# A scan's own-pixel term moved from VectorE passes to matrix products in PSUM

## The chip, the core and the metric

The kernel runs on one core of a Trainium2 chip. The metric is the device time of one execution in microseconds (us), the median of several runs. The core has five engines that run side by side and meet through semaphores: PE (TensorE: matrix products, which read SBUF and write PSUM; its weight loads are shown as PEld), DVE (VectorE), ACT (ScalarE), POOL (GpSimd) and SP (SyncE, which here issues the DMAs). Every array is float32.

## The reference

Four layers work on 32 images of 192 channels and 56 x 56 pixels, each of the form x = x + layer(group norm(x)): agent attention, a bidirectional RWKV scan, a shifted small convolution, and a long convolution by spectra. The change is in the second layer. Cut to what matters:

```python
k, v, r = xs @ Wk.T, xs @ Wv.T, xs @ Wr.T          # xs: the normalised image, one row per pixel
def wkv_scan(w, u, k, v):                           # over the pixels t, for each channel
    y[t]  = (p + exp(u + k[t]) * v[t]) / (q + exp(u + k[t]))
    p     = exp(w) * p + exp(k[t]) * v[t]
    q     = exp(w) * q + exp(k[t])
x_bi = 0.5 * (wkv_scan(forwards) + wkv_scan(backwards))
h    = layer_norm(sigmoid(r) * x_bi) * ln_g + ln_b
out  = h @ Wo.T
```

(The reference also carries a running maximum, left out here.) So at a pixel the numerator is the running sum p of the pixels before it plus exp(u) times its own term exp(k) v, and the denominator is the running sum q plus exp(u) times exp(k).

## The kernel before, in words

`all_blocks` runs, one after the other: `make_filter`, `attention` (over images), `scan_pairs` (the second layer), a guarded version of it that is skipped unless numbers overflow, and `channel_blocks` (third and fourth layer together). The change is within `scan_pairs`.

`scan_pairs` takes the images two at a time, 16 pairs. The 384 channels of a pair make three tiles of 128 partitions: the first 128 channels of either image, and the last 64 of both together. The 3136 pixels are cut into 4 pieces (m) of MC = 784, so a tile is 128 x 784, and as a PSUM bank holds 512 numbers, a product over a tile is two halves of 392 (HM). `turned()` hands out a PSUM buffer of two banks, one half in each; there are four such buffers.

Matrix products over channels go through `_Pairs`: `outer` makes the first two tiles, with a 128 x 128 block for each (L860) and a 64-row block for the shared tile (L863); `inner` makes the third, with a 128 x 128 block (L870) and 128 x 64 blocks (L873).

For each pair and piece there are three parts:

- `forwards`: normalised x (L1052, on ACT), key products and exp (L1101: ek = exp(k)), value products times ek (L1106: bv = exp(k) v), then for each tile `scan` forwards, `inverse` of the denominator, and the product num x den into y (L1113).
- `backwards`: normalised x again, the gate's products and its sigmoid as exp, ln, exp (L1126, L1130, L1131), `scan` backwards over the kept ek and bv, `inverse`, num x den (L1134), added to y (L1135) and times the gate (L1136).
- `finish`: centring products of y, squares (L1149), mean products, ln (L1158) and exp (L1168) for the layer norm, output products, the scale (L1169), the sum onto x (L1170), bn_stats of the result (L986), and the stores.

`scan` does the same twice, for p (from bv) and for q (from ek): POOL copies the carried value into the edge column of a fresh tile z of 785 columns (L1065), DVE runs the scan (L1070), POOL copies the last column out as the carry (L1071), and DVE makes `src * eu + before` in place over the columns "before" each pixel (L1072), with eu = exp(u) of each channel. `inverse` makes 1/den on ACT as exp(-ln den) (L1077, L1078), and keeps a sum of it for the overflow check. The z tiles have five buffers (tag pq), the x tiles seven, the tiles of tag t (gate, squares, rd) eight.

The main loop runs over pairs p. In each of its four turns it writes `backwards` of a piece of pair p, `finish` of the piece before it, `forwards` of a piece of pair p + 1, and in the first two turns `measure`, the moments of pair p + 2. No order is written by hand beyond that: a scheduler sets the order of each engine's instructions from the program's order, the dependences and the free buffers, once, when the kernel is built. On the chip each engine then runs its own list in that order, and waits for semaphores.

Before the loop the kernel multiplies Wo by the layer norm's gain and centres it, through PSUM and a scratch tensor in memory (`wogT`), and loads the constants.

Of the kernel before, what the change touches and what calls it, by code (L numbers as in the profile page):

```python
# [20 lines left out]
F32 = mybir.dt.float32  # L21
I32 = mybir.dt.int32
AF = mybir.ActivationFunctionType
ALU = mybir.AluOpType
# [4 lines left out]
C = 192  # L29
# [7 lines left out]
MC = 784  # L37
# [839 lines left out]
def scan_pairs(ctx: ExitStack, tc: tile.TileContext, a, k, x1, x2, rs2, wogT, count):  # L877
# [5 lines left out]
    nc = tc.nc  # L883
# [3 lines left out]
    wp = ctx.enter_context(tc.tile_pool(name="s_w", bufs=8))  # L887
# [5 lines left out]
    def small(name, shape):  # L893
        return cp.tile(shape, F32, name=name, tag=name)

    def turned():
        ps = pp.tile([128, 2, BANK], F32, name="ps", tag="ps")
        return ps, ps[:, :, :HM], [ps[:, h, :HM] for h in range(2)]

    def parts(t):  # L900
        return [t[:, h * HM : (h + 1) * HM] for h in range(2)]


    wo = [small("wo_a", [128, C]), small("wo_c", [64, C])]
    lg = [small("lg_a", [128, 1]), small("lg_c", [64, 1])]
    lb = [small("lb_a", [128, 1]), small("lb_c", [64, 1])]
    cen = [small("cen_a", [128, C]), small("cen_c", [64, C])]
    for i, r in enumerate((slice(0, 128), slice(128, C))):
        nc.sync.dma_start(out=wo[i], in_=a["L1_conv_WoT"][r])
        nc.sync.dma_start(out=lg[i], in_=a["L1_conv_ln_g"][r].unsqueeze(1))  # L910
# [3 lines left out]
    ps, _, _ = turned()  # L914
# [6 lines left out]
    for i, r in enumerate((slice(0, 128), slice(128, C))):  # L921
        n = (128, 64)[i]
        ps, _, _ = turned()
        for s in range(2):
            nc.tensor.matmul(ps[:n, 0, :C], cen[s][:, r], wo[s], start=(s == 0), stop=(s == 1))
        turn = wp.tile([128, C], F32, name="turn", tag="turn", bufs=1)
        nc.vector.tensor_copy(turn[:n], ps[:n, 0, :C])
        nc.sync.dma_start(out=wogT[r], in_=turn[:n])

    wk, wv, wr = (blocks(n, a[f"L1_conv_{n}T"]) for n in ("Wk", "Wv", "Wr"))  # L930
    wog, centre, mean_w, group = (
# [2 lines left out]
    wd = pairs.vector("wd", a["L1_conv_w_decay"])  # L934
    eu = pairs.vector("eu", a["L1_conv_u"])
    nc.scalar.activation(eu, eu, AF.Exp)

    w = small("w", [128, 2])
    nc.scalar.activation(w, wd, AF.Exp)
# [23 lines left out]
    def of(t):  # L963
        return slice(0, 1) if t < 2 else slice(1, 2)
# [42 lines left out]
    def deviations(st):  # L1007

        mv = moments(st)
        first, third = grouped([mv[:, t, 0:1] for t in range(3)])  # L1010
        mean = sp.tile([128, 3], F32, name="mean", tag="mean", bufs=4)
        nc.vector.tensor_copy(mean[:, 0:2], first)
        nc.vector.tensor_copy(mean[:, 2:3], third)
        d = sp.tile([128, 3], F32, name="d", tag="d", bufs=4)
        nc.vector.tensor_tensor(d, mv[:, :, 0], mean, ALU.subtract)
        nc.vector.tensor_tensor(d, d, d, ALU.mult)
        nc.vector.tensor_tensor(d, d, mv[:, :, 1], ALU.add)
        return mean, d

    def norm(mean, d):  # L1020

        first, third = grouped([d[:, t : t + 1] for t in range(3)])
        rs = sp.tile([128, 3], F32, name="rs", tag="rs", bufs=4)
        nc.vector.tensor_scalar(rs[:, 0:2], first, GN_EPS, None, ALU.add)
        nc.vector.tensor_scalar(rs[:, 2:3], third, GN_EPS, None, ALU.add)
        nc.scalar.activation(rs, rs, AF.Ln)
        nc.scalar.activation(rs, rs, AF.Exp, scale=-0.5)
        nb = sp.tile([128, 3], F32, name="nb", tag="nb", bufs=4)
        nc.vector.scalar_tensor_tensor(nb, mean, -1.0, rs, ALU.mult, ALU.mult)
        return mean, rs, nb  # L1030

    def stats_for(p):
        st = new_stats("st1")
        for m in range(NM):
            for t, x in enumerate(load(p, m)):
                stats_of(st, m, t, x)
        return st
# [11 lines left out]
    def normed(s, m):  # L1049
        xs = load(s.p, m)  # L1050
        for t in range(3):
            nc.scalar.activation(xs[t], xs[t], AF.Identity, bias=s.nb[:, t : t + 1], scale=s.rs[:, t : t + 1])  # L1052
        return [parts(t) for t in xs]

    def scan(s, m, t, carry, rev):

        b, e = s.bv[m][t], s.ek[m][t]
        c = eu[:, of(t)]
        got = []
        for i, src in enumerate((b, e)):  # L1060
            z = wp.tile([128, MC + 1], F32, name="pq"[i], tag="pq", bufs=5)
            edge, last = (MC, 0) if rev else (0, MC)
            out, before = (z[:, 0:MC], z[:, 1:]) if rev else (z[:, 1:], z[:, 0:MC])
            at = carry[t][i]
            nc.gpsimd.tensor_copy(z[:, edge : edge + 1], at)  # L1065
            if rev:
                out, data = out[:, ::-1], src[:, ::-1]
            else:
                data = src[:, :]
            nc.vector.tensor_tensor_scan(out, decay[:, of(t)].to_broadcast([128, MC]), data, at, ALU.mult, ALU.add)  # L1070
            nc.gpsimd.tensor_copy(at, z[:, last : last + 1])  # L1071
            nc.vector.scalar_tensor_tensor(before, src, c, before, ALU.mult, ALU.add)  # L1072
            got.append(before)
        return got

    def inverse(s, den, m, t, which):
        nc.scalar.activation(den, den, AF.Ln)  # L1077
        nc.scalar.activation(den, den, AF.Exp, scale=-1.0, accum_out=s.seen[:, which, 3 * m + t : 3 * m + t + 1])  # L1078

    def start(way):  # L1080
        carry = [[sp.tile([128, 1], F32, name=f"{way}{i}{t}", tag=f"{way}{i}{t}") for i in range(2)] for t in range(3)]
# [5 lines left out]
    def forwards(s, m):  # L1087
        s.ek[m] = [kp.tile([128, MC], F32, name="ek", tag="ek") for _ in range(3)]
        s.bv[m] = [kp.tile([128, MC], F32, name="bv", tag="bv") for _ in range(3)]
        s.y[m] = [kp.tile([128, MC], F32, name="y", tag="y", bufs=3 * NM + 4) for _ in range(3)]  # L1090
        xn = normed(s, m)
        for tiles in ((0, 1), (2,)):
            for wt in (wk, wv):
                ps = [turned() for _ in tiles]
                if len(tiles) == 2:
                    pairs.outer(wt, [q[2] for q in ps], xn)
                else:
                    pairs.inner(wt, ps[0][2], xn)
                for t, (_, both, _) in zip(tiles, ps):
                    if wt is wk:  # L1100
                        nc.scalar.activation(  # L1101
                            s.ek[m][t].rearrange("p (h n) -> p h n", h=2), both, AF.Exp,
                            accum_out=s.seen[:, 0, 3 * m + t : 3 * m + t + 1],
                        )
                    else:
                        nc.vector.tensor_tensor(  # L1106
                            s.bv[m][t].rearrange("p (h n) -> p h n", h=2), both,
                            s.ek[m][t].rearrange("p (h n) -> p h n", h=2), ALU.mult,
                        )
            for t in tiles:  # L1110
                num, den = scan(s, m, t, s.fore, False)
                inverse(s, den, m, t, 1)
                nc.vector.tensor_tensor(s.y[m][t], num, den, ALU.mult)  # L1113

    def backwards(s, m):
        xn = normed(s, m)
        h = s.y[m]
        for tiles in ((0, 1), (2,)):
            ps = [turned() for _ in tiles]
            if len(tiles) == 2:  # L1120
                pairs.outer(wr, [q[2] for q in ps], xn)
            else:
                pairs.inner(wr, ps[0][2], xn)
            for t, (_, both, _) in zip(tiles, ps):
                g = wp.tile([128, MC], F32, name="g", tag="t")
                nc.scalar.activation(  # L1126
                    g.rearrange("p (h n) -> p h n", h=2), both, AF.Exp, scale=-1.0,
                    accum_out=s.seen[:, 3, 3 * m + t : 3 * m + t + 1],
                )
                nc.scalar.activation(g, g, AF.Ln, bias=1.0)  # L1130
                nc.scalar.activation(g, g, AF.Exp, scale=-1.0)  # L1131
                num, den = scan(s, m, t, s.back, True)
                inverse(s, den, m, t, 2)
                nc.vector.tensor_tensor(num, num, den, ALU.mult)  # L1134
                nc.vector.tensor_tensor(h[t], h[t], num, ALU.add)  # L1135
                nc.vector.tensor_tensor(h[t], h[t], g, ALU.mult)  # L1136

    def finish(s, m):
# [59 lines left out]
    s, after, before = State(0, norm(*deviations(stats_for(0)))), norm(*deviations(stats_for(1))), None  # L1198
    for m in range(NM):
        forwards(s, m)  # L1200
    for p in range(last):
        ahead = State(p + 1, after) if p + 1 < last else None
        st = new_stats("st1")
        for i in range(NM):
            m = NM - 1 - i
# [20 lines left out]
        before, s = s, ahead  # L1226
# [16 lines left out]
    ps, _, _ = turned()  # L1243
# [568 lines left out]
```

## Time and profile before

| | us |
|---|---|
| median of 3 runs | 12,770.67 (12,757.16 to 12,775.48) |
| the profiled execution | 12,763.6 |
| its span | 12,761.8 |
| `make_filter` and `attention` | to about 5000 |
| `scan_pairs`, from its first key product to its last output product | 5081.6 to 8816.7 |
| `channel_blocks` | from about 8830 |

| busy in the span | us | share |
|---|---|---|
| PE | 11,522.3 | 90% |
| DVE | 11,221.3 | 88% |
| ACT | 5979.7 | 47% |
| POOL | 2199.4 | 17% |

The page shows one profiled execution. Its slices cut the span into 40 equal parts and give the busy share of each engine in tenths, and the clock that PE was granted in tenths of full speed. Groups of instructions are told by line, engine, operation and tile, with the number of records, the busy time and the mean duration of one. A product of float32 operands is two records, each with a weight load. Records of one engine overlap by some hundredths of a microsecond, so that what an instruction takes of its engine is read from start to start. The shares are means over three stages with different limits.

### The profile page before, as it was taken

What the parts mean: (1) busy time and instruction counts of PE and PEld (TensorE: products, weight loads), DVE (VectorE), ACT (ScalarE), POOL (GpSimd) and SP (SyncE); (2) the same over time, 40 slices, a digit from 0 to 9 for tenths busy, and PEclk for the clock granted to TensorE, in tenths of its full rate; (3) what the DMA queues carried; (4) which work ended last, traced back from release to release, by engine and by line L of the source; (5) the groups of instructions that cost most, each with busy time, mean ns of one, the idle gap of its engine ahead of it and who ended that gap; (6) DMA issues with size and microseconds to landing.
All of it is one profiled execution on the core that took longest, in us unless ns stands there. A gap on an engine that the chain in (4) does not pass through costs nothing. (4 is left out here: it accounts for less than half of the span.)

```text
span 12761.8 us, 165194 instructions
## 1 busy us (share of the span) xinstructions
PE 11522.3 (90%) x63158; PEld 7190.8 (56%) x63158; DVE 11221.3 (88%) x15929; ACT 5979.7 (47%) x11146; POOL 2199.4 (17%) x2238
## 2 busy tenths in 40 slices
PE   4999999999999997788878788787999999999999
PEld 1556555565555564333333333334777777777777
DVE  3888888888888886999999999998888888888888
ACT  2554554554554553555555555554333333333333
POOL 0000000000000000544445454544000000000000
PEclk8999999999999998889988899898999999999999
DMA  2111111111111112344443344433111111111111
GB/s 64 40 39 39 39 39 49 47 39 39 39 41 53 41 39 68 84 110 103 99 110 97 105 107 103 103 98 81 43 42 44 42 44 44 42 42 44 43 44 28
DMA packets 949574, 770.40 MB, mean 60 GB/s; under 512 B 769870, under 2 KB 811065, under 8 KB 939760
## 3 DMA queue, kind: packets, MB, share of 16 engines
q1 hardware_dynamic: 948776, 759.74, 22.7%
q8 instruction: 504, 8.26, 0.3%
q14 instruction: 294, 2.41, 0.1%
HBM read 479.96 MB, written 240.50 MB: 56 GB/s over the span
## 5 line engine op out<-in xcount | busy, mean ns | idle before, releaser
L589 DVE SCALAR_TENSOR_TENSOR o<-v_a,dww,o 128x896 f32<-128x896 f32 (+1 forms) x1024 | 1053.0, 1028 | 396.5 <-ACT v_a L563 314.2
L1739 ACT COPY y<-ps 64x252 f32<-64x252 f32 (+1 forms) x2376 | 806.4, 339 | 1132.6 <-PE ps L1733 1102.1
L1657 PE MATMUL ps<-f,real 84*84 84x112 f32 x6144 | 1090.8, 259 | 0.0
L1657 PE MATMUL ps<-f,imag 84*84 84x112 f32 x6144 | 1089.4, 259 | 0.0
L1664 ACT COPY z<-ps 84x448 f32<-84x448 f32 x768 | 405.0, 527 | 1219.9 <-PE ps L1657 1218.4
L1657 PEld LDWEIGHTS ps<-f,real 84*84 84x84 f32 x6144 | 783.9, 153 | 134.3 <-issue 95.8
L1084 POOL MEMSET f<- 128x1 f32 x96 | 8.8, 98 | 4810.6 <-PE ps L739 4805.6
L1077 ACT ACTIVATE q<-q 128x784 f32<-128x784 f32 x384 | 328.9, 857 | 999.1 <-DVE q L1072 753.0
L1657 PEld LDWEIGHTS ps<-f,imag 84*84 84x84 f32 x6144 | 763.8, 153 | 0.0
L606 ACT ACTIVATE pr<-ps,low 98x896 f32<-98x896 f32 (+1 forms) x384 | 351.9, 916 | 838.0 <-DVE low L604 838.0
L602 PE MATMUL ps<-xs_a,gk_a 128*98 128x448 f32 (+1 forms) x1536 | 637.8, 496 | 0.0
L589 DVE SCALAR_TENSOR_TENSOR o<-v_c,dww,o 128x448 f32<-128x448 f32 (+1 forms) x1024 | 634.1, 619 | 4.0
L603 PE MATMUL ps<-xs_c,gk_c 125*98 125x448 f32 (+1 forms) x1536 | 631.9, 492 | 0.0
L694 PE MATMUL ps<-gq_a,xs_a 128*112 128x294 f32 x1792 | 606.2, 419 | 19.2 <-DVE pq L699 19.2
L1674 PE MATMUL ps<-z,f 84*114 84x448 f32 x1536 | 608.9, 539 | 0.0
L695 PE MATMUL ps<-gq_c,xs_c 125*112 125x294 f32 x1792 | 596.4, 414 | 0.0
L1523 POOL TENSOR_TENSOR mat<-tap,tap 114x114 f32<-114x114 f32 x96 | 40.6, 423 | 3163.0 <-PE ps L1583 2310.0
L1631 PE MATMUL re<-y,f 128*84 128x420 f32 (+1 forms) x1152 | 532.0, 542 | 8.7 <-ACT y L1739 7.3
L1631 PE MATMUL im<-y,f 128*84 128x420 f32 (+1 forms) x1152 | 526.8, 538 | 0.0
L1733 PEld LDWEIGHTS ps<-f,padded 114*128 114x128 f32 x3168 | 471.5, 191 | 96.5 <-issue 70.4
L1733 PE MATMUL ps<-f,padded 114*128 114x168 f32 x3168 | 501.9, 310 | 21.4 <-DVE o L1676 10.0
L707 ACT ACTIVATE pq<-pq 112x1176 f32<-112x1176 f32 x224 | 265.3, 1184 | 525.1 <-DVE pq L699 401.9
(358 smaller groups left out, 29470.4 us busy)
## 6 DMA issues: line engine op xcount, KB each, us to landing
x<-x SPq DMA_DIRECT2D x640, 392.0 KB
x<-x SPq DMA_DIRECT2D x640, 196.0 KB
x<-x SPq DMA_DIRECT2D x192, 399.0 KB
out_x<-x SPq DMA_DIRECT2D x384, 196.0 KB
x_a<-in_x SPq DMA_DIRECT2D x32, 1568.0 KB
x<-x_a SPq DMA_DIRECT2D x32, 1568.0 KB
x_c<-in_x SPq DMA_DIRECT2D x64, 392.0 KB
x<-x_c SPq DMA_DIRECT2D x64, 392.0 KB
```

The costliest lines, as they stand in the source:

```text
L589: nc.vector.scalar_tensor_tensor(dst, tap(i), dww[:, t, i : i + 1], dst, ALU.mult, ALU.add)
L602: mm(ps[P2, h, :n], g[:, cols], xs_a[j][:, px], start=True, stop=False)
L603: mm(ps[P2, h, :n], gk_c[0:KC, 2 * j + h, cols], xs_c[j][0:KC, px], start=False, stop=True)
L606: nc.scalar.activation(pr[:, :, :n], ps[P2, :, :n], AF.Exp, bias=low[:, j, p : p + 1], accum_out=sums[:, j, p : p + 1])
L694: mm(ps[:SUB, i, :HA], xs_a[j][:, px], g, start=True, stop=False)
L695: mm(ps[:SUB, i, :HA], xs_c[j][0:KC, px], gq_c[0:KC, 2 * j + (q + i) // ns], start=False, stop=True)
L1631: nc.tensor.matmul(ps[:, : n * 84], f2[:, i, :], y[:, i0 : i0 + n].rearrange("p g s u -> p (g s u)"), start=True, stop=True)
L1657: nc.tensor.matmul(ps[:84, i * 2 * S : (i + 1) * 2 * S], part[:, i0 + i].rearrange("p s u -> p (s u)"), f3[:, m, :], start=(m == 0), stop= ...
L1664: nc.scalar.copy(z[:, i0 : i0 + n].rearrange("p g m w -> p (g m w)"), ps[:84, : n * 2 * S])
L1674: nc.tensor.matmul(got, f4[:, m, :], z[:, i0 : i0 + n, m, :], start=(m == 0), stop=(m == 1))
L1733: nc.tensor.matmul(ps[:, g * 168 : (g + 1) * 168], flat[:, (g0 + g) * 128 : (g0 + g + 1) * 128], f1, start=True, stop=True)
L1739: nc.scalar.copy(y[64 * m : 64 * m + 64, 2 * g0 + i : 2 * (g0 + n) : 2], got[64 * i : 64 * i + 64, :, :, m, :])
```

## The change: what it does

`scan` gives up L1072. Two diagonal matrices `own` (exp(u) on the diagonal, one for the first two tiles' channels and one for the third tile's) and an identity are made once. For q first and then for p, after the scan, PE multiplies the source by the diagonal into a fresh PSUM buffer and adds the identity times the "before" columns to it, each in two halves of 392 columns. For q, ACT reads the sum in PSUM, takes the logarithm into an SBUF tile (`y` itself forwards, a fresh tile of tag t backwards) and the exponential of its negative there; `inverse` is gone as a function. For p the sum stays in PSUM, and the product with 1/den reads it there.

The set-up's matrices (wo, cen, and the two halves of the turned Wo) no longer have buffers of their own but pass through the tiles of tag t; this makes room for the new constants.

```diff
+    def passing(n):
+        return wp.tile([128, MC], F32, name="passing", tag="t")[:n, :C]
...
-        turn = wp.tile([128, C], F32, name="turn", tag="turn", bufs=1)
+        turn = passing(n)
...
+    ident = small("ident", [128, 128])
+    nc.sync.dma_start(out=ident, in_=k["ident"])
+    own = [small(f"own{i}", [128, 128]) for i in range(2)]
+    for i in range(2):
+        nc.vector.tensor_scalar(own[i], ident, eu[:, i : i + 1], None, ALU.mult)
...
-    def scan(s, m, t, carry, rev):
+    def scan(s, m, t, carry, rev, den, which):
...
-        for i, src in enumerate((b, e)):
+        for i, src in ((1, s.ek[m][t]), (0, s.bv[m][t])):
...
             nc.gpsimd.tensor_copy(at, z[:, last : last + 1])
-            nc.vector.scalar_tensor_tensor(before, src, c, before, ALU.mult, ALU.add)
-            got.append(before)
-        return got
-
-    def inverse(s, den, m, t, which):
-        nc.scalar.activation(den, den, AF.Ln)
-        nc.scalar.activation(den, den, AF.Exp, scale=-1.0, accum_out=s.seen[:, which, 3 * m + t : 3 * m + t + 1])
+            _, both, halves = turned()
+            for w, rhs, first in ((own[of(t).start], src, True), (ident, before, False)):
+                for half, part in zip(halves, parts(rhs)):
+                    nc.tensor.matmul(half, w, part, start=first, stop=not first)
+            if i == 1:
+                nc.scalar.activation(den.rearrange("p (h n) -> p h n", h=2), both, AF.Ln)
+                nc.scalar.activation(
+                    den, den, AF.Exp, scale=-1.0, accum_out=s.seen[:, which, 3 * m + t : 3 * m + t + 1]
+                )
+        return both
...
-                num, den = scan(s, m, t, s.fore, False)
-                inverse(s, den, m, t, 1)
-                nc.vector.tensor_tensor(s.y[m][t], num, den, ALU.mult)
+                y = s.y[m][t]
+                num = scan(s, m, t, s.fore, False, y, 1)
+                y = y.rearrange("p (h n) -> p h n", h=2)
+                nc.vector.tensor_tensor(y, num, y, ALU.mult)
...
-                num, den = scan(s, m, t, s.back, True)
-                inverse(s, den, m, t, 2)
-                nc.vector.tensor_tensor(num, num, den, ALU.mult)
-                nc.vector.tensor_tensor(h[t], h[t], num, ALU.add)
+                den = wp.tile([128, MC], F32, name="den", tag="t")
+                num = scan(s, m, t, s.back, True, den, 2)
+                both = den.rearrange("p (h n) -> p h n", h=2)
+                nc.vector.tensor_tensor(both, num, both, ALU.mult)
+                nc.vector.tensor_tensor(h[t], h[t], den, ALU.add)
```

More of the change, by code (lines that the diff above doesn't have):

```diff
@@ L901, in parts @@
         return [t[:, h * HM : (h + 1) * HM] for h in range(2)]
-    wo = [small("wo_a", [128, C]), small("wo_c", [64, C])]
+    def passing(n):
+        return wp.tile([128, MC], F32, name="passing", tag="t")[:n, :C]
+    wo = [passing(128), passing(64)]
     lg = [small("lg_a", [128, 1]), small("lg_c", [64, 1])]
     lb = [small("lb_a", [128, 1]), small("lb_c", [64, 1])]
-    cen = [small("cen_a", [128, C]), small("cen_c", [64, C])]
+    cen = [passing(128), passing(64)]
     for i, r in enumerate((slice(0, 128), slice(128, C))):
@@ L925, in scan_pairs @@
             nc.tensor.matmul(ps[:n, 0, :C], cen[s][:, r], wo[s], start=(s == 0), stop=(s == 1))
-        turn = wp.tile([128, C], F32, name="turn", tag="turn", bufs=1)
-        nc.vector.tensor_copy(turn[:n], ps[:n, 0, :C])
-        nc.sync.dma_start(out=wogT[r], in_=turn[:n])
+        turn = passing(n)
+        nc.vector.tensor_copy(turn, ps[:n, 0, :C])
+        nc.sync.dma_start(out=wogT[r], in_=turn)
     wk, wv, wr = (blocks(n, a[f"L1_conv_{n}T"]) for n in ("Wk", "Wv", "Wr"))
@@ L1053, in normed @@
         return [parts(t) for t in xs]
-    def scan(s, m, t, carry, rev):
-        b, e = s.bv[m][t], s.ek[m][t]
-        c = eu[:, of(t)]
-        got = []
-        for i, src in enumerate((b, e)):
+    def scan(s, m, t, carry, rev, den, which):
+        for i, src in ((1, s.ek[m][t]), (0, s.bv[m][t])):
             z = wp.tile([128, MC + 1], F32, name="pq"[i], tag="pq", bufs=5)
```

## The prediction

> **What bounds the kernel now.** I read the page first: the slices show three stages. The change touches only the middle one, where POOL is busy (about slices 15 to 27).
>
> ```profile
> PE   4999999999999997788878788787999999999999
> DVE  3888888888888886999999999998888888888888
> POOL 0000000000000000544445454544000000000000
> PEclk8999999999999998889988899898999999999999
> ```
>
> In the middle stage DVE is full, and PE, at 7 to 8 tenths, is neither idle nor full; in the other stages it is PE that is full. The timeline of PE gives the stage's ends: the first key product starts at 5081.60 us, the last output product ends at 8816.7 us. The view by windows (us; busy us of PE, PEld, DVE, ACT, POOL; granted clock, DMA share, GB/s) sums it:
>
> ```profile
> 5081.60:8816.70 3735.10, 3031.53 (x10798) 1385.22 (x10796) 3657.67 (x4060) 2163.80 (x3578) 1862.21 (x1699) 0.90 0.40 101
> ```
>
> DVE works 97.9% of 3735 us: it is the bound. There are 16 pairs of images and 4 pieces each, so 64 steps of 58.36 us, each with one forward scan, one backward scan and one finish. What PE waits for is seen in its own waits between 5500 and 8000 us (42.8 steps):
>
> ```profile
> PE ps L860 <- ACT x L1052: 108.7, 14, 10.5
> PE ps L860 <- ACT sq L1149: 102.5, 37, 6.4
> PE ps L860 <- DVE rd L1169: 68.3, 48, 2.3
> PE ps L863 <- ACT x L1052: 59.1, 18, 5.8
> ```
>
> All ten rows of that view add to 457 us, 10.7 us a step. The other thing that inflates PE's busy time is its clock, 0.90 on the mean; in the stretch 6511.95 to 6514.70 us it was 0.54, in 6519.2 to 6522.0 it was 1.00.
>
> **What PE's work is at full clock.** At the stage's end PE runs a whole finish without a wait. Read the differences of the starts, not the durations, because records overlap; a matrix call shows as two records (four calls of L860 are "x8").
>
> ```profile
> 8797.59 2.90 PE L860 MATMUL ps<-y,cen_aa 128*128 128x392 f32 x8
> 8800.42 1.59 PE L863 MATMUL ps<-y,cen_ca 64*128 64x392 f32 x8
> 8801.94 1.58 PE L870 MATMUL ps<-y,cen_cc 128*128 128x392 f32 x4
> 8803.46 1.54 PE L873 MATMUL ps<-y,cen_ac 128*64 128x392 f32 x8
> 8804.92 2.90 PE L860 MATMUL ps<-sq,mean_aa 128*128 128x392 f32 x8
> ```
>
> Four full-array calls take 2.83 us and two take 1.52 us: 0.655 us a call and 0.2 us at each change of shape. The half-array calls (L863, L873) run two at a time, 1.52 and 1.46 us for four. A step has 6 groups of L860, 6 of L863, 5 of L870, 5 of L873: 17.0 + 9.1 + 7.6 + 7.3 = 41.0 us. The small group sums (four rounds of 1.8 us in four steps) add 1.8: 42.8 us a step. So PE has 58.4 - 42.8 = 15.6 us a step to spare: 10.7 of waits and some 4.9 of slow clock.
>
> **The change, part by part.**
>
> *Removed from DVE:* 12 instructions of L1072 a step, 768 in all.
>
> ```profile
> L1072 DVE SCALAR_TENSOR_TENSOR q<-ek,eu,q 128x784 f32<-128x784 f32 x384 | 391.8, 1024 | 0.5
> L1072 DVE SCALAR_TENSOR_TENSOR p<-bv,eu,p 128x784 f32<-128x784 f32 x384 | 386.5, 1020 | 0.0
> ```
>
> Their starts are 0.95 us from the next instruction's start (6516.18 to 6517.13), so DVE loses 12 x 0.95 = 11.4 us a step: 97.9% of 58.36 is 57.1, less 11.4 is 45.7 us. Were DVE still the bound, this would be worth 64 x 11.4 = 730 us.
>
> *Added on PE:* each scan call gets, for q and for p, two halves of a diagonal and two of an identity product: 8 calls, 6 scan calls a step, 48 calls, 3072 in all. The operands are 128x128 against 128x392 in f32, which is the form of L860: 48 x 0.655 = 31.4 us a step, 2011 us in all. Nothing makes them cheaper in the rows: L860 already repeats one weight matrix four times running, and its weight loads already lie beside the products. No change of shape is added, as the new runs stand where one shape already gave way to another. PE's step becomes 42.8 + 31.4 = **74.2 us**, against 45.7 us on DVE and 33.8 us (57.9% of 58.36) on ACT. The bound moves to PE; 64 x 74.2 = 4749 us is the floor of the stage, 1014 us above the 3735 it takes now.
>
> The Trainium skill bears on the price and is milder than the row: "TensorE: Matmul & The Clock Gate", section "Back-to-back issue gap", has a sustained stream of weight loads and products at about 131 ns for 512 columns, and "FP8 and Floating Point Precision", section "TensorE Precision Notes", has four passes for true FP32; that would be an estimated 0.40 us a call, 19.3 us a step, and a total near 13,260. The rows of L860 show 0.655 for this very form, in a stream of loads and products, at clock 1.00.
>
> *At nothing, and their cover:* ACT reads the denominators from PSUM (L1101 does so in 810 ns, L1077 from SBUF in 857). The last product on DVE reads a numerator in PSUM (L1106, 963 ns, against L1113, 961). Set-up: one more small load ahead of the x loads on SP, two tiny DVE products, passing buffers in place of constants; the stretch 5012 to 5055 us, where PE waits 41.8 us for the first moments, covers the building of the diagonals, and the added load may cost 0 to 10 us; I take 5. Two passing buffers for the two turned halves take a wait away that nobody stood behind.
>
> *New waits, and who queues behind them.* PE issues in order: diagonal q, identity q (after scan q), diagonal p (after bv), identity p (after scan p). Behind a late scan stands all of PE. For the forward scan I place the p scan: from the end of the value products DVE needs two bv (2 x 0.89) and a scan (1.76), 3.5 us; PE meanwhile has three pairs of the new calls, 3 x 1.31 = 3.9 us. It arrives just in time; if DVE first ends another scan, PE loses up to 1.4 us. In the backward scan ek and bv lie in SBUF and the scans run ahead, up to the five pq buffers. DVE's last product (L1113 and L1134 of before) now waits for PE and ACT, and behind it on DVE stand the next scans; DVE has 28 us a step of slack for that. A PSUM buffer of a numerator is held until this product; each of the four buffers comes round after three others, for the backward p two new pairs and the third tile's gate, 2.6 + 2.6 + 3.0 = 8.2 us, against some 2 us of ACT and 0.9 us of DVE. The edge columns copied by POOL (L1065, means 0.56 to 1.25 us, 12 a step, 11 us) now stand ahead of identity products instead of DVE work. All this is bounded by 0 and, with every edge copy paid in full, 11 us a step.
>
> *Waits that remain.* Between 0 and the whole 15.6 us of waits and slow clock. Those on sq, rd, g and bv (6.8 us a step) came from queues that ran late behind a full DVE; at the stage's end, with DVE nearly empty, the same chain shows no wait. They should go, and the clock with few gaps should stay near 1.00, as it does in the last stage (PE busy 98% of 8850 to 12700 us at 1.00). The wait for the normalised x, (108.7 + 59.1) / 42.8 = 3.9 us, comes from loads and their seven buffers, not from DVE: I keep it. So 74.2 + 3.9 = 78.1 us a step, 64 x 78.1 = 4998 us, 1263 more.
>
> **The sum.** The profiled execution took 12,763.6 us (span 12,761.8). 12,763.6 + 1263 + 5 = 14,032; the median of the runs lies 7 us above that execution, so **14,040 us**.
>
> **Rivals.**
> 1. *PE full, but with every hand-off paid* (chance 0.15). The five pq buffers, the four PSUM buffers and POOL's edge copies make PE wait 8 us a step or more. For it: POOL is busy 50% of the stage, and its copies wait for scans. Against: the buffers come round with several us to spare. With 3.9 + 11 us of waits: 89.1 us a step, 5702 us, a total of 14,740; with 8 us: 14,300.
> 2. *The new products are cheaper than L860* (0.03): constant weights save part of the work. Halfway to the price of a packed half-array call (1.52 / 4 = 0.38), 0.52 us: 42.8 + 25.0 + 3.9 = 71.7, a total of 13,630.
> 3. *Not slower* (0.02): the new products fill PE's spare 15.6 us and DVE's 11.4 us come free. The point is 15.6 / 48 = 0.325 us a call, half the row; only two calls sharing the array come near it, and a full 128x128 matrix leaves no half free. At 0.32 the time stays at 12,770; each 0.01 us below gives 31 us, until DVE's 45.7 us hold again.
>
> **How the numbers follow.** "PE is full, waits of 0 to 8 us a step" holds 0.80 and covers 13,780 (floor 1014 us and nothing else) to 14,300. The upper end goes to 14,450 (10.3 us of waits) to take in about half of rival 1; that leaves out under 2 in 10. A measurement of this kernel tells about 0.2% from no change; faster by more 0.01, within it 0.01, slower 0.98.
>
> **What would show it.** Right: in the middle stage PE at 9 tenths and more at a clock near 1.00, DVE at 6 tenths, the new line with 6144 records of one matrix form whose starts are 0.65 us a call apart, no L1072-like DVE work, and a stage of about 5000 us; the outer stages as they were. Wrong in size: PE's waits on DVE scans, on POOL copies or on numerators' products above 8 us a step, or a clock that stays at 0.90 (74.2 / 0.90 + 3.9 = 86.3 us a step, 14,570). Wrong altogether: new calls under 0.33 us.

## The result: slower by 9%, PE is full

The changed kernel takes 13,925.6 us (median of 4, 13,917.2 to 13,933.1) against 12,771.2 us: the ratio is 1.0906, 95% interval 1.0887 to 1.0925. The prediction was 14,040 (13,780 to 14,450). The profiled execution took 13,923.9 us, its span 13,921.8.

The slices of the page after, to be laid beside those of before:

```profile
PE   4999999999999979999999999999899999999999
DVE  4888888888888866666666666665688888888888
POOL 0000000000000001111111111111200000000000
PEclk7999999999999989999999999999999999999999
```

In the middle stage PE and DVE have changed places: PE is at 9 and DVE at 6 tenths, and PE's clock is full. The outer stages are as they were: what follows the scan stage takes 3949 us, against 3945. The scan stage, first key product to last output product, now lasts 4884 us, 76.3 us a step in place of 58.4. Its row in the view by windows (us; busy us of PE, PEld, DVE, ACT, POOL; granted clock, DMA share, GB/s):

```profile
5088.60:9972.60 4884.00, 4804.73 (x16942) 2450.91 (x16940) 3058.18 (x3291) 2229.99 (x3578) 669.84 (x1699) 1.00 0.31 77
```

PE is busy 4805 of 4884 us, 98.4%, about what DVE was before (97.9%); DVE is at 63%. PE's view of waits for the stage has three rows (us in total, times, longest), 76 of PE's 79 us of idle time:

```profile
PE ps L1081 <- DVE bv L1115: 43.7, 27, 1.7
PE ps L1081 <- DVE p L1076: 31.1, 30, 1.1
PE ps L860 <- DVE rd L1180: 1.1, 3, 0.8
```

The eleven such rows of before summed to 701 us. The price of a new call is read from PE's timeline in the backward part:

```profile
7507.61 1.58 PE L1081 MATMUL ps<-ek,own 128*128 128x392 f32 x4
7509.03 1.48 PE L1081 MATMUL ps<-q,ident 128*128 128x392 f32 x4
7510.35 1.48 PE L1081 MATMUL ps<-bv,own 128*128 128x392 f32 x4
7511.67 1.48 PE L1081 MATMUL ps<-p,ident 128*128 128x392 f32 x4
```

Four records are two calls, and the starts are 1.32 us apart (1.42 behind the change of shape): 0.66 us a call, as on L860.

### The profile page after: what moved, and what is told of

Same layout as the page of the kernel before. It is cut to its first block, busy times and chain, and to the rows that moved or that the text cites. A ratio compares the mean times of both kernels' runs of the same rounds, so it can differ in the third digit from the quotient of the medians.

```text
span 13921.8 us, 177262 instructions
## 1 busy us (share of the span) xinstructions
PE 13306.6 (96%) x69302; PEld 8265.3 (59%) x69302; DVE 10621.3 (76%) x15163; ACT 6046.4 (43%) x11146; POOL 1007.4 (7%) x2238
## 5 line engine op out<-in xcount | busy, mean ns | idle before, releaser
L995 DVE BATCH_NORM_STATS2 st<-x 128x6 f32<-128x392 f32 x768 | 389.3, 556 | 369.0 <-DMA x<-x 366.3
L1081 PE MATMUL ps<-bv,own 128*128 128x392 f32 x1536 | 570.1, 494 | 43.7 <-DVE bv L1115 43.7
L1081 PE MATMUL ps<-p,ident 128*128 128x392 f32 x1536 | 573.4, 495 | 32.9 <-DVE p L1076 31.1
L1081 PE MATMUL ps<-ek,own 128*128 128x392 f32 x1536 | 594.9, 510 | 0.0
L1076 DVE TENSOR_TENSOR_SCAN p<-decay,b,bv 128x784 f32<-128x784 f32 x192 | 353.8, 1843 | 308.6 <-PE ps L1081 308.0
L1081 PE MATMUL ps<-q,ident 128*128 128x392 f32 x1536 | 570.8, 493 | 1.3
L1061 ACT ACTIVATE x<-x,nb,rs 128x784 f32<-128x784 f32 x384 | 396.3, 1033 | 389.8 <-DMA x<-x 313.4
```

Source lines behind the costliest of these rows:

```text
L1081: nc.tensor.matmul(half, w, part, start=first, stop=not first)
```

## The experiments

The theory: the stage follows the sum of the fuller engine, PE after the change and DVE before it. The rivals: hand-offs through few buffers set the step, or the order of q and p does. All ratios are against the kernel before.

### More and fewer products

Every diagonal product twice:

```diff
-            for w, rhs, first in ((own[of(t).start], src, True), (ident, before, False)):
+            for w, rhs, first, last_ in ((own[of(t).start], src, True, False), (own[of(t).start], src, False, False), (ident, before, False, True)):
```

> The changed kernel with every diagonal product issued twice (each sum then holds the pixel's own term twice): 24 more full-array calls a step, 1536 in all. Theory (PE is full, a call takes 0.655 us): 24 x 0.655 x 64 = 1006 us more than 13,926, so 14,930, within 40. Rival (hand-offs between PE, ACT and DVE set the step, and PE's work lies partly in their shadow): less than half of it, under 14,430. Rival (repeated weights are cheaper): in between, and starts less than 0.6 us apart in the trace.

Measured: 14,832.8 us, 907 more than the changed kernel (ratio 1.1616, 1.1593 to 1.1640). The stage's row:

```profile
5075.09:10874.40 5799.31, 5797.96 (x20014) 3046.46 (x20012) 3065.58 (x3291) 2231.73 (x3578) 481.81 (x1699) 0.99 0.26 65
```

PE's busy time grew by 993 us, 0.647 us for each of 1536 calls, and its idle time fell from 79 us to 1.4: 993 - 78 = 915, the stage's growth. The time is 97 us below the 14,930 expected, outside its 40: the sum left out that the last waits vanish (78 us), and a call took 0.647 us, not 0.655 (13 us). Both rivals are out. A call has its full price when it is issued twice, and hand-offs have next to nothing left to hide or add: this is what a full engine looks like.

The diagonal product of the numerators left out:

```diff
-            for w, rhs, first in ((own[of(t).start], src, True), (ident, before, False)):
+            terms = ((own[of(t).start], src), (ident, before))[1 - i :]
```

> The changed kernel without the diagonal product of the numerators (p then lacks the pixel's own term): 12 calls a step fewer, 768 in all; the scans, the identity products and all of ACT's and DVE's work stay. Theory (PE full): 12 x 0.655 x 64 = 503 us less, 13,420; up to 60 us more if the wait for the p scan, which the diagonal product covered, opens. Rival (hand-offs set the step): the time stays above 13,800.

Measured: 13,520.0 us, 406 less (ratio 1.0588, 1.0567 to 1.0609), 40 us above the theory's upper end and far below the rival. PE's largest wait in the stage:

```profile
PE ps L1082 <- DVE p L1076: 128.8, 121, 3.3
```

It is four times that of the changed kernel: the diagonal product had covered the p scan. PE's idle time grew by 60 us, and with it came 140 us at half clock in place of 44. So PE begins to leave the bound at some 70 us a step.

### DVE's work put back

```diff
+            spare = wp.tile([128, MC], mybir.dt.bfloat16, name="spare", tag="spare", bufs=1)
+            nc.vector.scalar_tensor_tensor(spare, src, eu[:, of(t)], before, ALU.mult, ALU.add)
             _, both, halves = turned()
```

> The changed kernel with the removed instruction put back on DVE as spare work, 12 a step, after each scan, into a tile that nobody reads (bf16, for want of space): DVE gets 12 x 0.95 = 11.4 us a step more, 48 + 11 = 59 of some 76 us. Theory (PE full, DVE has slack): within 0.5% of 13,926, a little more at the forward p scan, which then comes up to 1 us later (64 x 3 x 1 us = 190 us at the very most). Rival (scans handed from DVE to PE set the step): 400 to 730 us more.

Measured: 14,080.2 us, 155 more than the changed kernel (ratio 1.1028, 1.1010 to 1.1047): 1.1%, outside the 0.5% and inside the "at the very most". DVE is busy 710 us more, and only a fifth of it shows. The stage is 157 us longer: PE is idle 76 us more, nearly all of it in the same two waits as after the change (146 us in place of 75, shown below), and busy 81 us more, of which 133 us at half clock in place of 44 explain some 45. The remaining 36 us or so were not taken apart.

```profile
PE ps L1083 <- DVE bv L1117: 75.0, 50, 2.7
PE ps L1083 <- DVE p L1076: 70.7, 107, 1.1
```

Read against the kernel before, this run is the change without its removal: the products on PE, with q ahead of p and the sums read from PSUM, cost 12,771 to 14,080, 1309 us, and the work taken from DVE then gives 155 back.

### DVE's work taken away, with nothing added

```diff
-            nc.vector.scalar_tensor_tensor(before, src, c, before, ALU.mult, ALU.add)
+            if i == 1:
+                nc.vector.scalar_tensor_tensor(before, src, c, before, ALU.mult, ALU.add)
```

> The kernel before without the removed instruction for the numerators (p then lacks the pixel's own term), 6 of 12 a step, and nothing added on PE. Theory (DVE is the bound of the kernel before): 64 x 6 x 0.95 = 365 us less than 12,770, so 12,405, within 60. Rival (the two engines' in-order lists, not DVE's sum, set the step of before): less than 130 us of gain.

Measured: 12,589.9 us, 182 less than before (ratio 0.9859, 0.9839 to 0.9879): half of the theory's gain, and above the rival's limit. DVE is busy 332 us less, and idle 230 us in place of 77. What it waits for now, in the stage:

```profile
DVE rd L1170 <- ACT rd L1169: 122.5, 49, 3.1
DVE rd L1170 <- PE ps L863: 50.2, 13, 10.8
```

Before, the first of these was 15.4 us. So DVE was the bound, but with little behind it: a few microseconds a step below, the chain of the finish (centring, squares, mean, ln, exp, scale) holds DVE's list. For the 730 us that the prediction gave for DVE's whole saving, had DVE stayed the bound, this speaks against having them in full: half of the instructions gave half of their price. All twelve were not taken away.

### The order of q and p

In the changed kernel, p ahead of q again (the loop's two sources exchanged):

> The changed kernel with p ahead of q in the scan, as before the change. Theory (PE full, the order is of little weight): PE's calls are the same, so within 0.5% of 13,926; PE may wait some 1 to 3 us a step for the bv product and the p scan, which now stand directly behind the value products (64 to 190 us more at most). Rival (q ahead is what keeps PE full): over 300 us more.

Measured: 14,212.4 us, 287 more (ratio 1.1132, 1.1113 to 1.1150), above the theory's 190 and just below the rival's 300. PE's waits in the stage:

```profile
PE ps L1081 <- DVE bv L1117: 249.1, 128, 4.4
PE ps L1081 <- DVE p L1076: 36.6, 100, 0.4
```

The numerator's product stands right behind the value products, and bv stands on DVE behind scans: 3.9 us a step. Idle time grew by 218 us, and PE's busy time by 72, with 201 us at half clock in place of 44. So q ahead of p is worth 2% to the changed kernel, and it is what made its waits so few.

In the kernel before, the same exchange and nothing else:

```diff
-        for i, src in enumerate((b, e)):
+        for i, src in ((1, e), (0, b)):
...
-            got.append(before)
+            got.insert(0, before)
```

> The kernel before with nothing but q ahead of p in the scan. Theory (DVE is full there, and its work is the same): within 0.5% of 12,770; the denominators' logarithm starts up to 2.8 us earlier, which takes away DVE's waits for it (33 us in all in the stage). Rival (the order is a part of the change that helps or hurts by itself): over 0.5% either way.

Measured: 12,720.3 us against 12,773.8 (ratio 0.9963, 0.9948 to 0.9977), 53 us less. DVE's largest wait of before is gone from its list:

```profile
DVE p L1134 <- ACT q L1078: 37.1, 42, 1.5
DVE rd L1169 <- ACT rd L1168: 15.4, 19, 1.9
```

(these two are of before; the second is 1.7 us now). The denominator's logarithm and exponential get done while DVE makes the numerator. DVE's idle time in the stage falls from 77 to 30 us, which is the stage's whole gain of 46 us. The gain of 0.4% is within the theory's 0.5% and clear of the interval: this part of the change helps by itself, and this kernel is faster than both.

### A part of the scans on PE

If the fuller engine set the step, a mixture should beat both kernels. The changed kernel with a condition ahead of the products, and the old instruction otherwise:

```diff
+            if t == 2:
                 _, both, halves = turned()
...
+            else:
+                nc.vector.scalar_tensor_tensor(before, src, eu[:, of(t)], before, ALU.mult, ALU.add)
+                both = before.rearrange("p (h n) -> p h n", h=2)
```

The other conditions are `i == 1 and rev`, `i == 1` and `i == 1 and not rev`.

> The changed kernel, but only the third tile's scans (p and q, both ways: 4 of the 12 a step) go through PE; the other 8 keep the instruction of before on DVE. Theory (the step is that of the fuller engine): DVE 57.1 - 4 x 0.95 = 53.3 us, PE 75.1 - 8 x 2.62 = 54.1 us a step; with 1 to 2 us of waits 55 to 56 us against 58.4 before: 64 x -2.4 to -3.4, so 12,550 to 12,620. Rival (two engines that are both nearly full wait for each other in turn): over 12,700, no gain.

> The changed kernel, but only the backward denominators (3 of the 12 a step) go through PE. Theory: DVE 57.1 - 3 x 0.95 = 54.3 us, PE 75.1 - 9 x 2.62 = 51.5 us; DVE stays the bound at 98%: 55.4 us a step, 12,580, within 40. Rival (both nearly full): over 12,700.

> The changed kernel, but only the denominators (6 of the 12 a step) go through PE, the numerators keep the instruction on DVE. Theory: DVE 57.1 - 6 x 0.95 = 51.4 us, PE 75.1 - 6 x 2.62 = 59.4 us, the bound: with 1 to 2 us of waits 60.4 to 61.4 a step, 12,900 to 12,965. Rival (hand-offs of the numerators were what cost, the denominators ride along with ACT): 12,770 or less.

| on PE, of 12 a step | us | ratio | against the kernel with q first, per instruction moved |
|---|---|---|---|
| 0 (q first) | 12,720.3 | 0.9963 | |
| 3, backward q | 12,936.5 | 1.0127 (1.0110 to 1.0144) | 72 |
| 4, third tile | 13,096.7 | 1.0256 (1.0239 to 1.0273) | 94 |
| 6, all q | 13,249.1 | 1.0373 (1.0353 to 1.0394) | 88 |
| 12, all | 13,925.6 | 1.0906 | 100 |

The theory fails here: none gains, and each misses its expected time by 280 us and more; the third tile and the backward q are in the range of their rival, two nearly full engines that wait for each other, and all q is far above its own. With three moved, PE (3532 of 3898 us busy) and DVE (3488) are both short of full. The timeline shows how, first PE and then DVE of the kernel with the backward q on PE:

```profile
7009.74 1.59 PE L863 MATMUL ps<-x,Wr_ca 64*128 64x392 f32 x8
7015.39 2.98 PE L1082 MATMUL ps<-ek,own 128*128 128x392 f32 x4 [4.06 <-ACT g L1140]
7018.16 1.51 PE L870 MATMUL ps<-x,Wr_cc 128*128 128x392 f32 x2
7019.46 1.93 PE L1082 MATMUL ps<-q,ident 128*128 128x392 f32 x4
```

```profile
7038.03 0.30 DVE L1197 COPY row<-mean 128x168 f32<-128x168 f32 x1
7043.60 1.85 DVE L1184 TENSOR_TENSOR rd<-ps,rd 128x784 f32<-128x784 f32 x2 [5.27 <-PE ps L863]
```

PE stands 4 us before a new product, reaches the output products late, and DVE, at the end of its scans, stands 5.3 us before their scale with the next scans behind it. Over the stage DVE lost 226.5 us at this place. It lost another 157.7 us before the statistics of freshly loaded x (6.2 us in the kernel before), where the loads came later than DVE asked:

```profile
DVE rd L1184 <- PE ps L863: 226.5, 38, 11.1
DVE st L995 <- DMA x<-x: 157.7, 55, 4.5
```

PE's 4 us are not for a scan: ek was made in the forward part, and what ends the wait is ACT's reading of the gate out of PSUM, so the product seems to have lacked one of the four PSUM buffers. Over the stage the diagonal products wait 74 us in this way, and the identity products 111 us for scans:

```profile
L1082 PE MATMUL ps<-q,ident 128*128 128x392 f32 x768 | 341.8, 573 | 122.8 <-DVE q L1076 111.4 <-DVE d L1024 10.0 <-DVE d L1026 0.2
L1082 PE MATMUL ps<-ek,own 128*128 128x392 f32 x768 | 328.4, 556 | 74.0 <-ACT g L1140 52.2 <-DVE bv L1119 21.0
```

To see whether the place matters, the forward q instead:

> As the kernel with only the backward denominators on PE, but the forward ones instead (3 of 12 a step). Sums: DVE 54.3 us, PE 51.5 us, which as a maximum gave 12,580 and was wrong for the backward ones (12,936). New theory (an identity product blocks PE's list until its scan is done on a DVE that is full; PE then reaches the output products late, and DVE's list stands before their scale): the forward scan of q lies a value product ahead, so less of it, 12,600 to 12,850. Rival (whatever is moved to PE costs some 72 us per instruction of a step, wherever it stands): 12,900 to 12,980.

Measured: 12,917.4 us (ratio 1.0111, 1.0094 to 1.0128), in the rival's range: of these two places neither is cheaper, and my new theory that the forward one is cheaper is wrong. The stage shows a like pair of waits, of PE (here for the scan itself) and of DVE:

```profile
PE ps L1082 <- DVE q L1076: 227.8, 48, 6.8
...
DVE rd L1184 <- PE ps L863: 208.8, 37, 9.1
```

That two in-order lists stop each other in turn is read from these rows, and no run shows it apart from the buffers: the number of PSUM buffers and of x tiles was left as it was. Whether more of them, or another order of the lists, would win the time back was not tried, and stays open.

### Fewer scan buffers

In the changed kernel `tag="pq", bufs=3` in place of 5.

> The changed kernel with three scan buffers in place of five. Theory (hand-offs have slack, PE is full): PE uses up one buffer in 2.6 us and DVE fills one in 1.8, so the backward scans still keep ahead: 0 to 200 us more. Rival (the buffers were what kept PE fed, as in the first rival of the prediction): over 500 us more, with PE's waits on scans at 8 us a step and more.

Measured: 13,927.2 us, the same as the changed kernel (ratio 1.0906, 1.0884 to 1.0928), and PE's waits are the same to 1 us. With PE full the scan buffers have slack, so this part of the prediction's first rival has no ground. The PSUM buffers, its other part, were not varied; that PE waits 1.2 us a step in all, and not 8, speaks against it.

### The small group sums

In the changed kernel, their right side and output widened from one column to 128:

```diff
-            nc.tensor.matmul(ps[:, t, 1:2], group[0], src[t], start=True, stop=False)
+            nc.tensor.matmul(ps[:, t, 0:128], group[0], wide[t], start=True, stop=False)
```

> The changed kernel with the small group sums of the moments made over 128 equal columns in place of one (the same sums, 127 of them thrown away). After these runs of small products the gate's products took 4.6 us in place of 2.9 at a granted clock of 0.62 in the changed kernel, although PE's records show no gap. Theory (products of one column do not count as activity for the clock): no such 4.6 us any more, PE's clock at 1.00 there, 20 to 60 us less than 13,926. Rival (the clock falls for another reason): the 4.6 us stay, and the time is the same or up to 50 us more.

Measured: 13,954.6 us, 29 more (ratio 1.0928, 1.0910 to 1.0947). The clock's part of the theory holds, its time does not: 20 to 60 us less were expected. In the changed kernel, then in the one with wide sums:

```profile
7565.97 0.28 PE L873 MATMUL ps<-d,grp_ac 128*64 128x1 f32 x4
7566.19 4.59 PE L860 MATMUL ps<-x,Wr_aa 128*128 128x392 f32 x8
```

```profile
7576.65 0.44 PE L873 MATMUL ps<-d,grp_ac 128*64 128x128 f32 x4
7577.02 2.90 PE L860 MATMUL ps<-x,Wr_aa 128*128 128x392 f32 x8
```

Behind its first few microseconds the stage then has no stretch at half clock, but a wide product takes 0.41 us where a narrow one takes 0.31: all of them together are busy 163 us in place of 123, which costs more than the 22 us that 44 us at half clock are worth.

## Why the prediction was right, step by step

- **PE becomes the bound, at L860's price.** Right: 0.66 us a call from the starts, 0.647 from doubling; 75.1 us a step busy against a floor of 74.2. The rival "cheaper than L860" and the rival "not slower" (under 0.325) are both out, and so is the milder estimate of 0.40 us a call, with its total near 13,260.
- **The clock returns to full speed.** Right: granted 1.00 in the stage, 44 us at half clock in place of 710.
- **The x wait of 3.9 us a step is kept.** Wrong in size and in cause, and the term that makes the difference: PE no longer waits for the normalised x at all. I took the loads as its cause because DVE does not make x. ACT makes it, and in the kernel before ACT's own list stood behind DVE. Between 5500 and 8000 us nearly the whole wait falls at one place in each pair, the gate's products. There are ten of these, all alike; one of them, first PE, then ACT:

```profile
7551.48 1.54 PE L873 MATMUL ps<-x,Wv_ac 128*64 128x392 f32 x8
7563.48 5.60 PE L860 MATMUL ps<-x,Wr_aa 128*128 128x392 f32 x8 [10.46 <-ACT x L1052]
7573.98 2.98 PE L863 MATMUL ps<-x,Wr_ca 64*128 64x392 f32 x8 [4.91 <-ACT x L1052]
```

```profile
7560.66 0.86 ACT L1077 ACTIVATE q<-q 128x784 f32<-128x784 f32 x1 [6.27 <-DVE q L1072]
7561.55 0.86 ACT L1078 ACTIVATE q<-q 128x784 f32<-128x784 f32 x1
7562.31 0.19 ACT L1078 ACTIVATION_READ_ACCUMULATOR q<-q 128x1 f32 x1
7562.40 1.96 ACT L1052 ACTIVATE x<-x,nb,rs 128x784 f32<-128x784 f32 x2
7567.80 0.86 ACT L1077 ACTIVATE q<-q 128x784 f32<-128x784 f32 x1 [3.44 <-DVE q L1072]
```

  ACT reaches x only after a denominator's logarithm, which waits for L1072 on the full DVE, so this was a wait of the kind that I expected to go. Loads had a small part at most: in the kernel before without the numerators' instruction ACT waits 7.4 us for loads in the stage, and PE still 208 us for x; in the changed kernel ACT waits 304 us for them (177 before), and PE not at all. The waits of PE that are left, 1.2 us a step, are the two that the walk through the forward part had named and the sum had put at nothing, bv and the p scan. The stage has 76.3 us a step and not 78.1: 1.8 x 64 = 115 us, the distance from 14,040 to 13,926. This 1.8 is a net: 3.9 us went, and 1.2 of waits and 0.9 of PE's work above the floor came, so the time lies nearer to the forecast than this term does, by luck.
- **DVE at 45.7 us, ACT at 33.8, PSUM reads at nothing.** Nearly right: 47.8 (DVE's busy time fell by 600 us, not by 730) and 34.8, far from the bound.
- **POOL's edge copies ahead of identity products.** Bounded by 0 and 11 us; measured 0: no PE wait on POOL is listed.
- **Set-up 5 us.** Not resolved: the stage starts 7 us later, but in the runs with this set-up it starts anywhere from 5075.1 to 5095.5 us, and in those without it from 5068.7 to 5081.6.
- **730 us if DVE had stayed the bound.** Too much, as far as was tried: in the kernel without the numerators' instruction half of the price of six instructions is lost to the next chain.

## What to carry to other kernels

Before work is moved to an engine that "has time", price it by the nearest shape on that engine, start to start at full clock, and add it to that engine's sum of the stage: a busy share of 81% held 10.7 us of waits a step, and the moved work needed 31.4. An engine's saving is worth its sum only down to the next limit, and a mixture of two nearly full engines in fixed order reaches neither sum. Take a change apart before judging it: here the removal gave little, the addition cost 1309 us, and the smallest part, q ahead of p, gained by itself in both kernels.

## What the runs showed of the hardware

A run of one-column products, with no gap in PE's records from 7562.75 to 7566.19 us, was followed by a stretch of half clock (granted 0.62 over the next 4.5 us); with 128 columns it was not:

```profile
7562.70:7566.20 3.50, 3.50 (x30) 3.27 (x28) 1.20 (x3) 1.04 (x1) 0.22 (x2) 1.00 0.02 5
7566.20:7570.70 4.50, 4.50 (x10) 2.18 (x8) 2.38 (x9) 0.41 (x2) 0.28 (x2) 0.62 0.00 0
```

The length of the run matters: from 5400 us to the end of the changed kernel's stage 13 such runs last 3.4 us or more, and each is followed by one half-clock stretch of 3.41 us; 32 runs of half that length (1.7 us) are followed by none. In the kernel with the diagonal products twice, where PE is idle 1.4 us in the whole stage, 13 half-clock stretches of 3.41 or 6.83 us stand behind such runs as well. The Trainium skill ("TensorE: Matmul & The Clock Gate", section "Part 1: The HAM clock gate") has the clock fall after an idle window of about 3.4 us. The half-clock stretches within the stages of these traces are 3.41 us and multiples of it; but PE's records show no idle window here, so one-column products did not keep the clock up.

POOL's copies of one column took longer beside a fuller DVE. The carry of q backwards, before, after, and with the diagonal products twice (busy us, mean ns):

```profile
L1071 POOL COPY b<-q 128x1 f32<-128x1 f32 x192 | 297.3, 1548 | 25.2 <-DVE q L1070 13.4 <-DVE d L1016 0.2
```

```profile
L1077 POOL COPY b<-q 128x1 f32<-128x1 f32 x192 | 124.4, 648 | 565.9 <-DVE q L1076 395.3 <-DVE d L1025 69.6 <-DVE d L1024 52.2
```

```profile
L1077 POOL COPY b<-q 128x1 f32<-128x1 f32 x192 | 40.6, 212 | 572.9 <-DVE q L1076 399.4 <-DVE d L1025 66.5 <-DVE d L1024 52.2
```

The same copy takes 1.55, 0.65 and 0.21 us as DVE's share of the stage goes from 98% to 63% and 53%. The share alone does not set it: without the numerators' diagonal product the copy takes 0.20 us, at 68%. As the copy is the same in all of them, most of its time before was not work of its own, and POOL's 50% of that stage was no load of that size. What makes it wait was not taken apart.
